# Cross attention's scores: products divided by head into two column tiles, in one run per step behind a gate on both query tiles

## The chip, the core and the metric

The kernel runs on one core of a Trainium2 chip. The core has a matrix engine (TensorE; the profile calls its matmuls PE and its weight loads PEld), a vector engine (DVE), a scalar engine (ACT), GpSimd (POOL), and SyncE (SP), which here only issues DMA transfers. The metric is the time of one execution on the device in microseconds.

## What is computed

One decoder layer on x of 16 x 64 x 512 in fp32, in three parts, each added to its input after a layer norm: attention across the batch, cross attention to a context of the same shape, and a mixture of experts (16 experts, 4 for each token, and one shared expert). The change is in the cross attention:

```python
H, KVH, HD = (32, 8, 128)
q = (hidden_states @ Wq.T).reshape(bsz, q_len, H, HD).transpose(0, 2, 1, 3)
...
q = _rmsnorm(q, q_norm_w)
...
scores = jnp.einsum('bhqd,bhkd->bhqk', q, k) * scale
scores = scores + attention_mask[:, :, :, :kv_len]
probs = jax.nn.softmax(scores.astype(jnp.float32), axis=-1).astype(q.dtype)
out = jnp.einsum('bhqk,bhkd->bhqd', probs, v)
...
return out @ Wo.T
```

There are 16 sequences of 64 queries and 64 keys, 32 query heads of 128 elements, and 8 key heads, each for a group of 4 query heads.

## The kernel before

The 1024 tokens are 8 tiles of 128, that is two sequences to a tile. Batch attention (`batch_attention`, lines 306 to 364) comes first, with the keys and values (`keys`, `values`) made in between. Cross attention follows in steps: `cross` (line 583) goes through pairs (g, u), with g one of 8 groups of 4 heads and u one of 4 pairs of tiles, so there are 32 steps. Groups 0 to 5 go one after the other; in the last eight steps groups 6 and 7 alternate, and the layer norm and the routing for the experts (`normed_pair`, `routed_pair`, `entered`) are mixed in.

A step does the following, in the order of the program:

- `softmaxed`: for both tiles of the pair, `normed_queries` scales the raw queries by their inverse root (DVE, line 479), turns them with four transposes on PE (line 482) into a bank of PSUM, and writes them to `qt` in SBUF on ACT with the norm's weight (line 484). `qt` has two buffers and is laid out as [element, sequence of the tile, head, query]. Then come the score products (line 499): for each of two pairs of heads and each of two sequences, one product whose stationary operand is `qt` of two heads x 64 queries (128 columns) and whose moving operand is the 64 keys of that sequence. Its result fills 128 partitions (two heads x 64 queries) and 64 columns of the bank `sc`. Eight products fill the 512 columns. The softmax follows on DVE and ACT (lines 504 to 515).
- `queries`: makes the raw queries of a later step, by seven products of half size in place of eight (`seven`, line 254), and their squares on ACT (line 466).
- `projected`: the output projection of the step before, again seven products (line 254).
- `attended`: turns the probabilities (line 521), multiplies them with the values (line 531, in two row tiles of 64: `64*128` in the profile) and copies the result (line 537).

An fp32 product is two records on PE, two passes each with its own weight load; a transpose is one. Tiles are handed out from pools, and the order of the instructions on each engine is laid down when the program is built, by a scheduler that takes from what is ready by its own timing the first in the program's order. So PE's order in the profile is not the program's: products of `queries` fill in where transposes or scores aren't ready. On the chip each engine then goes through its instructions in that fixed order and waits where an operand isn't there.

For comparison: batch attention's last product (line 358) writes its two halves h to two column tiles of 64 (`128*64` in the profile), and its first (line 327) works on two row tiles (`64*128`).

Of the kernel before, what the change touches and what calls it, by code (L numbers as in the profile page):

```python
# [26 lines left out]
ALU = mybir.AluOpType  # L27
AX = mybir.AxisListType

P = 128  # L30
N, C, L = 16, 64, 512
# [11 lines left out]
SURE = 32  # L43
WB = 4
ROUND = float(3 << 22)


@with_exitstack
def decoder_layer(
# [25 lines left out]
    V, S, T, G = nc.vector, nc.scalar, nc.tensor, nc.gpsimd  # L75
# [17 lines left out]
    def tr_bank():  # L93
        return bank("tr", 2)

    def sc_bank():
        return bank("sc", 3)
# [6 lines left out]
    kT = [p.tile([P, KVH // 2, NT * P], F32, tag="kT", name="kT") for p in (kvp0, kvp)]  # L104
# [372 lines left out]
    def normed_queries(g, i):  # L477
        raw = q_raw.pop((g, i))
        V.tensor_mul(raw, raw, q_rs[g, i // 2][:, i % 2, :].unsqueeze(2).to_broadcast([P, GRP, HD]))  # L479
        tp = tr_bank()  # L480
        for j in range(GRP):
            T.transpose(tp[:, j * P : (j + 1) * P], raw[:, j, :], ident)
        qt = work.tile([P, 2, GRP, C], F32, tag="qt", name="qt", bufs=2)
        S.activation(  # L484
            qt.rearrange("p b h q -> p h b q"),
            tp.rearrange("p (h b q) -> p h b q", h=GRP, b=2), AF.Copy, scale=qw_sb,
        )
        return qt

    def softmaxed(g, u):  # L490
        sp = sc_bank()
        for j in range(2):
            i = 2 * u + j
            qt = normed_queries(g, i)
            for hp in range(2):
                for b in range(2):
                    k0 = i * P + b * C
                    at = ((j * 2 + hp) * 2 + b) * C
                    T.matmul(  # L499
                        sp[:, at : at + C], qt[:, b, 2 * hp : 2 * hp + 2, :],  # L500
                        kT[g // 4][:, g % 4, k0 : k0 + C], start=True, stop=True,
                    )
        pr = work.tile([P, 8, C], F32, tag="prob", name="prob")
        V.scalar_tensor_tensor(  # L504
            pr, sp.rearrange("p (a k) -> p a k", a=8), HD**-0.5,
            mask_sb.unsqueeze(1).to_broadcast([P, 8, C]), ALU.mult, ALU.add,
        )
        mx = small.tile([P, 8], F32, tag="mx", name="mx")
        V.tensor_reduce(mx, pr, AX.X, ALU.max)
        V.tensor_sub(pr, pr, mx.unsqueeze(2).to_broadcast([P, 8, C]))  # L510
        S.activation(pr, pr, AF.Exp)
        sm = small.tile([P, 8], F32, tag="sm", name="sm")
        V.tensor_reduce(sm, pr, AX.X, ALU.add)
        V.reciprocal(sm, sm)
        V.tensor_mul(pr, pr, sm.unsqueeze(2).to_broadcast([P, 8, C]))
        return pr
# [66 lines left out]
    def cross(steps):  # L583
        for g, u in steps:
            if u == 1 and g + 2 < KVH:
                load_wq(g + 2)
            if u == 0 and g + 1 < KVH:
                load_wo(g + 1)
            pr = softmaxed(g, u)
            if g < KVH - 2:  # L590
                queries(*divmod(NT // 2 * g + u + 3, NT // 2))
            elif g == KVH - 2:
                queries(g + 1, u)
            if (g, u) == (KVH - 3, NT // 2 - 1):
                queries(g + 1, u)
            if late:
                projected(*late.pop())
            late.append((g, u, *attended(g, u, pr)))
            if g == KVH - 2 and u > 0:
                summed(u - 1)  # L600
                normed_pair(u - 1)
                if u > 1:
                    entered(u - 2, 1)
            if g == KVH - 1 and u > 0:
                routed_pair(u - 1)
                entered(u - 1, 0)
            if (g, u) == (KVH - 2, 0):
                load_shared(0)
            if (g, u) == (KVH - 2, NT // 2 - 1):
                load_shared(1)  # L610
# [78 lines left out]
    def routed_pair(u):  # L689
# [65 lines left out]
        V.tensor_scalar(col, got, 1.0 / P, (P - 1) / (2.0 * P), ALU.mult, ALU.subtract)  # L755
        V.tensor_scalar(col, col, ROUND, ROUND, ALU.add, ALU.subtract)
        row = route.tile([P, 2 * TOPK], F32, tag="row", name="row", bufs=1)
# [333 lines left out]
```

## Time and profile before

| | |
|---|---|
| median of 3 runs | 1028.77 us (1027.92 to 1031.83) |
| profiled execution | 1028.65 us, span 1026.6 us |
| PE busy | 976.3 us (95%), 4568 matmuls |
| PEld busy | 685.3 us (67%) |
| DVE busy | 542.1 us (53%) |
| ACT busy | 436.1 us (42%) |
| POOL busy | 328.7 us (32%) |
| granted TensorE clock, mean | 0.988 |

Times are from the start of the span. A row of the order of time gives start, length, engine, line, operation, out<-in, the tile of the array (rows*columns used), and in brackets the idle time before it and who ended it; xN are N records merged, so its length runs from the first start to the last end. A row of a group gives busy time and the mean ns of one, then the idle time of the engine just before. A matmul record lasts from its start to its modelled end and overlaps the next, so starts tell more than lengths.

### The profile page before, as it was taken

The numbers are of one execution on the slowest core, as the hardware profiler recorded it, in microseconds if no ns is written. First come the engines' busy times: TensorE is split into PE (matmuls) and PEld (weight loads), VectorE is DVE, ScalarE is ACT, GpSimd is POOL, SyncE is SP. The second block draws the span as 40 slices with busy tenths as digits, with TensorE's granted clock in tenths as the row PEclk, the third lists the DMA queues.
The fourth block names the chain that finished last, engine by engine and source line by source line (L and its number), as shares of the span: only waits on it lengthen the run. The fifth ranks groups of instructions, "written<-read, shape, count | busy, mean of one in ns | idle before, by whom it ended". The sixth has DMA issues, their size and how long they took to land. (4 is left out here: it accounts for less than half of the span.)

```text
span 1026.6 us, 13682 instructions
## 1 busy us (share of the span) xinstructions
PE 976.3 (95%) x4568; PEld 685.3 (67%) x4568; DVE 542.1 (53%) x1156; ACT 436.1 (42%) x1153; POOL 328.7 (32%) x356
## 2 busy tenths in 40 slices
PE   8999998999999999999999999988899999999994
PEld 3456555788888888887888887776654454454542
DVE  3555757664845756647458567688675211111110
ACT  2366662665454545545545464344220222222221
POOL 2132111421613516135235142032052444444433
PEclk9999999999999999999999999999899999999998
DMA  9120015200201102012010010000024966655764
GB/s 233 67 93 21 11 39 116 83 1 1 83 1 42 42 1 82 1 52 82 1 46 39 15 68 1 21 22 22 21 62 145 361 153 147 150 100 132 184 171 80
DMA packets 28954, 76.80 MB, mean 75 GB/s; under 512 B 4624, under 2 KB 9024, under 8 KB 26832
## 3 DMA queue, kind: packets, MB, share of 16 engines
q1 hardware_dynamic: 18160, 52.96, 15.5%
q0 software_dynamic: 10432, 22.66, 10.9%
q8 instruction: 38, 0.62, 0.3%
q14 instruction: 36, 0.29, 0.1%
q10 hardware_dynamic: 288, 0.26, 0.1%
HBM read 102.31 MB, written 14.97 MB: 114 GB/s over the span
## 5 line engine op out<-in xcount | busy, mean ns | idle before, releaser
L954 PE MATMUL sc<-w,xt 128*128 128x512 f32 x288 | 130.2, 593 | 0.3 <-ACT xt L947 0.3
L466 ACT ACTIVATE square<-qraw 128x128 f32<-128x128 f32 x256 | 79.2, 309 | 75.8 <-DVE qraw L460 37.6
L228 POOL TENSOR_TENSOR sat<-at 128x256 f32<-128x256 f32 x24 | 19.9, 828 | 211.8 <-ACT at L537 211.8
L954 PEld LDWEIGHTS sc<-w,xt 128*128 128x128 f32 x288 | 51.8, 190 | 51.7 <-issue 51.2
L959 DVE TENSOR_TENSOR z<-sc,z 128x256 f32<-128x256 f32 x36 | 15.3, 425 | 123.5 <-ACT z L958 116.7
L499 PEld LDWEIGHTS sc<-kT,qt 128*128 128x128 f32 x512 | 61.7, 191 | 17.5 <-ACT qt L484 9.3
L254 PE MATMUL mm<-wq_t,xns 128*128 128x256 f32 x256 | 70.5, 385 | 2.9 <-POOL wq_t L236 1.8
L254 PE MATMUL mm<-wo_sb,at 128*128 128x256 f32 x256 | 67.4, 388 | 5.4 <-ACT at L537 5.4
L254 PE MATMUL mm<-wq_sb,xnT 128*128 128x256 f32 x256 | 70.4, 381 | 0.0
L974 PE MATMUL mm<-w,zt 128*128 128x512 f32 x144 | 68.0, 594 | 1.5 <-DVE zt L967 1.0
L499 PE MATMUL sc<-kT,qt 128*128 128x64 f32 x512 | 69.0, 280 | 0.0
L254 PE MATMUL mm<-wo_t,sat 128*128 128x256 f32 x256 | 67.5, 384 | 0.6 <-DVE sat L229 0.6
L982 POOL DMA_INDIRECT out_dram<-y,idx x36 | 57.4, 1593 | 32.4 <-DMA out_dram<-y,idx 25.0
L936 POOL DMA_INDIRECT xg<-rows_d,idx x40 | 39.7, 994 | 82.2 <-PE tr L965 52.6
L504 DVE SCALAR_TENSOR_TENSOR prob<-sc,mask_sb 128x512 f32<-128x512 f32 x32 | 22.0, 689 | 81.4 <-PE sc L499 81.4
L479 DVE TENSOR_TENSOR qraw<-qraw,rs 128x512 f32<-128x512 f32 x64 | 62.4, 1011 | 0.6
L782 POOL DMA_INDIRECT table_d<-entry_sb,at_slot x24 | 26.0, 1084 | 108.5 <-DVE at_slot L749 102.1
L958 ACT ACTIVATE z<-sc 128x256 f32<-128x256 f32 x36 | 13.8, 384 | 104.4 <-PE sc L954 101.3
L254 PEld LDWEIGHTS mm<-wo_sb,at 128*128 128x128 f32 x256 | 48.7, 193 | 13.6 <-ACT at L537 7.2
L254 PEld LDWEIGHTS mm<-wo_t,sat 128*128 128x128 f32 x256 | 48.4, 192 | 7.3 <-POOL wo_t L237 0.7
L254 PEld LDWEIGHTS mm<-wq_t,xns 128*128 128x128 f32 x256 | 46.8, 190 | 8.7 <-POOL wq_t L236 2.0
L974 PEld LDWEIGHTS mm<-w,zt 128*128 128x128 f32 x144 | 27.1, 190 | 35.3 <-issue 32.0
(274 smaller groups left out, 2058.5 us busy)
## 6 DMA issues: line engine op xcount, KB each, us to landing
w<-in_wg_dram SPq DMA_DIRECT2D x40, 512.0 KB
w<-in_wu_dram SPq DMA_DIRECT2D x40, 512.0 KB
w<-in_wd_dram SPq DMA_DIRECT2D x40, 512.0 KB
wq_sb<-in_wq_dram SPq DMA_DIRECT2D x8, 1024.0 KB
wo_sb<-in_wo_dram SPq DMA_DIRECT2D x8, 1024.0 KB
xs<-in_x_dram SPq DMA_DIRECT2D x8, 256.0 KB
wv_sb<-in_wv_dram SPq DMA_DIRECT2D x2, 1024.0 KB
ct<-in_ctxt_dram SPq DMA_DIRECT2D x8, 256.0 KB
```

The lines of the kernel that those rows point to most:

```text
L228: engine.tensor_add(s[:, 0], a21, a22)
L254: T.matmul(dst, left[:, k, :], right[:, k, :], start=k == 0, stop=k == 1)
L466: S.activation(square, raw[:, h, :], AF.Square, accum_out=q_ss[g][:, 2 * u + j, h : h + 1])
L479: V.tensor_mul(raw, raw, q_rs[g, i // 2][:, i % 2, :].unsqueeze(2).to_broadcast([P, GRP, HD]))
L499: T.matmul(sp[:, at : at + C], qt[:, b, 2 * hp : 2 * hp + 2, :], kT[g // 4][:, g % 4, k0 : k0 + C], start=True, stop=True,)
L504: V.scalar_tensor_tensor(pr, sp.rearrange("p (a k) -> p a k", a=8), HD**-0.5, mask_sb.unsqueeze(1).to_broadcast([P, 8, C]), ALU.mult, ALU.add,
L782: G.indirect_dma_start(tables_d[q], bass.IndirectOffsetOnAxis(at_slots[u][:, q : q + 1], axis=0), entry_sb[:, 2 * u + j, k, :], None,)
L936: G.indirect_dma_start(xg, None, rows_d, bass.IndirectOffsetOnAxis(idx[:, b : b + 1], axis=0))
L954: T.matmul(hp, xt[:, d, :], w1_tiles[buffer(j)][:, :, d, :], start=(d == 0), stop=(d == DC - 1))
L959: V.tensor_mul(z, hp[:, FI:], z)
L974: T.matmul(op, zt[:, c, :], w2_tiles[buffer(j)][:, c, :], start=(c == 0), stop=(c == FI // P - 1))
L982: G.indirect_dma_start(out, bass.IndirectOffsetOnAxis(idx[:, b : b + 1], axis=0), y, None, bounds_check=NT * P - 1, oob_is_err=False, comp ...
```

## The change

```diff
+LOWEST = -3.0e38
...
     def softmaxed(g, u):
         sp = sc_bank()
-        for j in range(2):
-            i = 2 * u + j
-            qt = normed_queries(g, i)
-            for hp in range(2):
-                for b in range(2):
-                    k0 = i * P + b * C
+        qts = [normed_queries(g, 2 * u + j) for j in range(2)]
+
+        first, second = (qt[:, :, :, 0:1] for qt in qts)
+        V.scalar_tensor_tensor(first, second, LOWEST, first, ALU.is_ge, ALU.mult)
+        for hp in range(2):
+            for b in range(2):
+                for j, qt in enumerate(qts):
+                    k0 = (2 * u + j) * P + b * C
                     at = ((j * 2 + hp) * 2 + b) * C
-                    T.matmul(
-                        sp[:, at : at + C], qt[:, b, 2 * hp : 2 * hp + 2, :],
-                        kT[g // 4][:, g % 4, k0 : k0 + C], start=True, stop=True,
-                    )
+
+                    for h in range(2):
+                        T.matmul(
+                            sp[h * C : (h + 1) * C, at : at + C], qt[:, b, 2 * hp + h, :],
+                            kT[g // 4][:, g % 4, k0 : k0 + C], start=True, stop=True,
+                        )
```

Each product of two heads becomes two of one head: 64 stationary columns in place of 128, the same 64 keys as moving operand, and the result in the lower or the upper 64 partitions, which makes the two heads two column tiles. The products of both tiles of the pair come after both tiles' queries. Between them stands one DVE instruction, the gate: on one query of each head and sequence (8 elements of each partition) it multiplies the first tile's values by (second tile's value >= -3.0e38), which is 1, and writes them back in place. So the first tile's products wait for the gate and the gate waits for the second tile's `qt`; the second tile's products wait for their `qt` alone. Results and their places stay the same.

## Prediction

> **What bounds the kernel now.** I first cut the span into stages and took each engine's busy time in each. The columns are the stretch, its length, then busy time and instruction count of PE, PEld, DVE, ACT and POOL, the granted TensorE clock, the DMA share and GB/s.
>
> ```profile
> core 0: us, PE busy (x) PEld busy (x) DVE busy (x) ACT busy (x) POOL busy (x), PEclk, DMA share, GB/s
> 190.00:460.00 270.00, 266.99 (x1486) 226.91 (x1486) 164.38 (x281) 142.51 (x412) 95.35 (x106) 1.00 0.09 33
> 460.00:725.00 265.00, 249.84 (x1397) 211.30 (x1396) 185.94 (x389) 128.31 (x348) 81.23 (x78) 0.99 0.09 33
> ```
>
> Cross attention runs from 190 to about 727 us. PE is busy in 516.8 of these 535 us at full clock; DVE, the next engine, in 350. As busy ends of matmuls are modelled, I checked the order of time in one ordinary step (the lines of PE and of what it waits for):
>
> ```profile
> 506.37 0.60 PE L482 MATMUL tr<-ident,qraw 128*128 128x128 f32 x4
> ...
> 506.80 0.60 PE L254 MATMUL mm<-wq_sb,xnT 128*128 128x256 f32 x2
> ...
> 507.33 1.13 PE L531 MATMUL sc<-pt,v 64*128 64x256 f32 x8
> ...
> 508.39 1.10 PE L499 MATMUL sc<-kT,qt 128*128 128x64 f32 x8
> ...
> 509.34 0.61 PE L482 MATMUL tr<-ident,qraw 128*128 128x128 f32 x4
> ...
> 509.78 0.60 PE L254 MATMUL mm<-wq_sb,xnT 128*128 128x256 f32 x2
> ...
> 509.98 0.69 ACT L484 ACTIVATE qt<-tr,qw_sb 128x512 f32<-128x512 f32 x1 [0.36 <-PE tr L482]
> ...
> 510.21 0.59 PE L254 MATMUL mm<-wq_t,xns 128*128 128x256 f32 x2
> ...
> 510.72 0.97 PEld L499 LDWEIGHTS sc<-kT,qt 128*128 128x128 f32 x8 [0.31 <-ACT qt L484]
> 510.72 1.10 PE L499 MATMUL sc<-kT,qt 128*128 128x64 f32 x8
> ...
> 511.86 0.69 DVE L504 SCALAR_TENSOR_TENSOR prob<-sc,mask_sb 128x512 f32<-128x512 f32 x1 [5.04 <-PE sc L499]
> ```
>
> Each PE row starts as the one before drains; the step repeats every 16.58 us (L531 at 507.33 and at 523.91) without a hole. So in an ordinary step PE's own issue is the bound, and a nanosecond taken from it comes off the end. DVE meanwhile stands idle 5 us for the scores.
>
> The score products themselves, with the DVE row nearest to the gate:
>
> ```profile
> L499 PEld LDWEIGHTS sc<-kT,qt 128*128 128x128 f32 x512 | 61.7, 191 | 17.5 <-ACT qt L484 9.3 <-issue 8.0
> L499 PE MATMUL sc<-kT,qt 128*128 128x64 f32 x512 | 69.0, 280 | 0.0
> L758 DVE SCALAR_TENSOR_TENSOR row<-col,got 128x8 f32<-128x8 f32 x1 | 0.2, 156 | 0.0
> ```
>
> The 256 products of the code give 512 records, two passes each. Record by record they start 111 ns apart. A 256-wide record (L254) takes 216 ns and a 128-wide one (L482) 109, that is width times 0.84 ns, so 64 columns need 54 ns: the 128-column weight load, 107 ns, is the bound here and half the matmul slot is empty. That is what a column tile can win.
>
> **The nearest row for the new form.** Batch attention already has column tiles of 64 (L358, 128*64, alternating between the halves), with 128 moving columns. First PE's rows around it, then the first loads of that run in a window of 80 ns:
>
> ```profile
> 63.77 0.43 PE L358 MATMUL sc<-pt,qt 128*64 128x128 f32 x2
> 64.14 0.66 PE L318 MATMUL tr<-ident,xf 128*128 128x128 f32 x4
> 64.72 1.09 PE L358 MATMUL sc<-pt,qt 128*64 128x128 f32 x14
> 65.74 1.16 PE L327 MATMUL sc<-xf 64*128 64x128 f32 x16
> ```
> ```profile
> 64.72 0.20 PEld L358 LDWEIGHTS sc<-pt,qt 128*64 128x64 f32 x4 [0.16 <-ACT pt L353]
> ```
>
> Fourteen records in 1.09 - 0.27 = 0.82 us are 63 ns apiece, where one tile alone would need 109. Record by record, partners on the two halves start 7 ns apart and a pair repeats every 109 ns: both tiles run at full width at once. The four loads start at 0, 6, 55 and 61 ns: a 64-column load takes 54 ns, and the halves load at the same time; on one path the fourth would have started at 160 ns.
>
> **Part by part.**
>
> *Twice as many products, half as wide.* A step has 16 records of 128 columns now, 32 of 64 columns afterwards, 16 on each half. With load and matmul both 54 ns per tile, plus the 3 or 4 ns that L499 shows over its load, a pair takes 57 ns: 16 x 57 = 0.91 us, in place of 16 x 111 = 1.78. A rule speaks against this: the Trainium skill, "TensorE: Matmul & The Clock Gate", Part 3, "The mechanism", says that loads overlap matmuls in flight only where the row group differs, and both halves here use all 128 rows. By the rule a record would cost load plus matmul, 107 ns, the run 3.4 us and the kernel 32 x 1.9 = 60 us more (estimate). But L358 shares its rows too, and its loads start inside matmuls in flight; I take the row.
>
> *Changes of tiling.* Between L318 and L358 the start-to-start is 203 ns in place of 109, out as well as in: 94 ns. The first record of a new form also doesn't overlap its load: 160 ns in place of 109 for L318 (+0.05), 320 in place of 216 for L254 (+0.105). Now a step changes form for L531 alone; afterwards also into and out of the score run. New per step: in 0.094, first pair 0.05, out 0.09, first L254 after it 0.105, and 0.058 for transposes that come right behind L531 where the scores stood: 0.40 us. What goes: 0.08 us that L254 gives up ahead of the second half's scores (291 ns in place of 216), and the same first-record losses of L499, 2 x 0.05.
>
> *Sum of a step.* Before: 0.942 + 0.941 (the two score runs to the next row's start) + 0.075 = 1.96. After: 0.91 + 0.40 = 1.31. Saved 0.65. In the six steps whose scores already are one run of 16: 1.835 + 0.07 = 1.905 before, 1.25 after, the same 0.65. Times 32: 20.9 us.
>
> *The gate.* One DVE instruction a step, 128x8, between the second tile's L484 on ACT and the first tile's scores. Nearest row L758, 156 ns; L514, 128x8, has 192. With some 0.03 from ACT to DVE and 0.05 from DVE to PE (read at L442 to L443, and L479 to L482) it adds 0.25 us to the way from queries to scores. Queued behind it on DVE stand L504 and the softmax, which wait for these scores anyway, and in a group's first steps L479 of later tiles. As DVE waited for the scores in 25 of 32 steps (81.4 us in all), its 32 x 0.17 = 5.5 us cost DVE nothing there. On PE the L254 products fill the wait, as four do now in 509.78 to 510.72; the second tile's scores wait for ACT alone and may go ahead of the first's. Without that cover the gate costs its 0.25 us each step, 8 us. Lower end: zero, since the drain of the change of form (0.09) runs beside it; a gain is excluded. Upper end: 0.3 us in each step, 9.6. I take 0.06 a step, 2 us, nearer to the covered steps.
>
> *Where PE isn't the bound.* In the last eight steps (from 586 us) PE has about 12 us of waits for chains through DVE and ACT. There I count half: 2.6 us less. No DMA is issued or moved; both qt buffers are used in a step as before, and the softmax that follows starts at about the same point (it ends at 517.0 in the step shown, and L521, which needs it, comes at 522.5).
>
> Sum against the profiled execution (1028.65 us, of which 1026.6 are span): 20.9 - 2.6 - 2.0 = 16.3 saved. It lies 0.1 us from the median of the runs, 1028.77, so I forecast 1012.5.
>
> **Rivals.**
>
> *Slower: the pairs don't keep up.* L358 shows two loads and two matmuls in 109 ns; the change asks for that in 57, twice the rate. If PE gives out one matmul with its load no faster than about L358's own 55 to 63 ns, the halves take turns. The same skill page, Part 1, "Wait — 56ns, not 53.3ns?", has a sequencer cost of 62 ns a matmul when the hardware decoder is off, and a floor of 25 ns otherwise: by the first, 32 x 62 + 400 = 2.38 us a step, 13.5 us slower in all (estimate); by the second nothing changes. At 57.5 ns it is 2.24, 0.28 a step, 9 us slower: 1038. It decides from 49 ns a record, where 32 x 49 + 400 meets 1.96. For it: no row is denser. Against it: starts 6 and 7 ns apart at the head of each run, which no such floor allows. Chance 0.15.
>
> *Little gained: the run is late or cut up.* The order on each engine is fixed before the run from another timing than the chip's. If PE stands 0.4 us for the gate (a 1.0 us L479 ahead of it on DVE, half seen), or the run is cut in two (another 0.34 us of changes), 0.3 or less of the 0.65 is left: 32 x 0.25 = 8 us at most, with the late steps' loss some 5: 1024. For it: L479 rows of a group's start stand five together. Against it: 25 idle waits of DVE. Chance 0.17.
>
> *The gain is given back later.* The routing and expert stages (from 727 us) wait on this stage's end only, so they move with it; I see nothing that would hold them. Chance 0.03, about 1027.
>
> **How the numbers follow.** My forecast, 1012.5, has 0.65; its own range is 1006 (no losses, 20.9 saved, and a little more in the late steps) to 1019 (gate at its upper end). Cutting off the slower case and a low tail leaves 1005 to 1030. Half a per cent, 5.1 us, is about what a measurement can tell from no change. Faster by more: the 0.65 and half of the second rival, 0.74; within: 0.11; slower: 0.15.
>
> **What would show it.** In the changed profile the score rows should be 128*64, 1024 records, some 32 in one stretch of about 1.2 us (the last record's tail included), once a step; two or more stretches a step would be the second rival, 1.9 us or more the first. A step should repeat every 15.9 us. PE's idle ahead of the scores, put down to DVE, should stay under 0.1 us a step, and DVE's wait at L504 should shrink by what it waits at the gate. I am wrong if the stretch is long, if PE waits for the gate, or if other products are moved so that L521 waits for the softmax.

## The result, and the profile after

The changed kernel takes 1055.42 us (median of 6 runs, 1053.76 to 1056.35), the kernel before 1028.35 in its 6 runs beside it: a ratio of 1.0254, with a 95% interval of 1.0233 to 1.0274. The profiled execution took 1056.17 us, of which 1054.3 are span, at a mean granted clock of 0.969 (0.988 before). That is 27 us slower where I had forecast 16 us faster, and far outside my range.

In the changed code most lines of this stage stand five further down: the scores are L504 (L499 before), the scaling of the raw queries L480 (L479), their transposes L483 (L482), the copy to `qt` L485 (L484), the first softmax instruction L509 (L504), the projections' products L255 (L254), the products with the values L536 (L531), the copies of their results L542 (L537). The gate is L496.

The stages, with the columns of the table in the prediction:

```profile
190.00:460.00 270.00, 249.54 (x1654) 207.10 (x1653) 169.21 (x286) 133.73 (x389) 91.93 (x92) 0.97 0.08 28
460.00:725.00 265.00, 240.09 (x1547) 198.11 (x1545) 174.19 (x343) 120.84 (x336) 78.10 (x83) 0.95 0.10 34
```

PE is idle for 20 us of the first stretch, where it was idle for 3, and its granted clock is 0.97 and 0.95, where it was 1.00 and 0.99. The groups of the score products and of the gate (busy us, mean ns, then the idle time of the engine just before them) say for whom it stood:

```profile
L504 PE MATMUL sc<-kT,qt 128*64 128x64 f32 x1024 | 40.2, 237 | 25.7 <-DVE qt L496 25.7
L496 DVE SCALAR_TENSOR_TENSOR qt<-qt 128x8 f32<-128x8 f32 x32 | 11.9, 371 | 49.4 <-ACT qt L485 49.3
```

The tiles are as planned: 1024 records, 40.2 us of PE in place of 69.0. But PE waits 25.7 us for the gate, 26 times, where its score rows had 0.0 us of idle time ahead of them. Where that is lies in the order of time. An ordinary step first, PE's rows of one from behind the second tile's transposes to the scores (the step repeats every 16.19 us, L536 at 504.98, 521.17 and 537.36; 16.58 before):

```profile
522.72 0.60 PE L255 MATMUL mm<-wq_sb,xnT 128*128 128x256 f32 x2
523.16 1.03 PE L255 MATMUL mm<-wq_t,xns 128*128 128x256 f32 x4
524.41 1.15 PE L504 MATMUL sc<-kT,qt 128*64 128x64 f32 x32 [0.23 <-DVE qt L496]
```

All 32 records stand in one run of 1.15 us, next row at 525.49, and PE waits 0.23 us. Here the change gains. Now the second step of a group, here of group 2. First PE, then DVE:

```profile
340.23 0.55 PE L483 MATMUL tr<-ident,qraw 128*128 128x128 f32 x3 [1.08 <-DVE qraw L480]
...
343.76 0.59 PE L255 MATMUL mm<-wq_sb,xnT 128*128 128x256 f32 x2
348.13 1.97 PE L504 MATMUL sc<-kT,qt 128*64 128x64 f32 x32 [3.78 <-DVE qt L496]
350.04 2.08 PE L255 MATMUL sc<-wq_sb,xnT 128*128 128x256 f32 x4
```
```profile
338.38 1.79 DVE L480 TENSOR_TENSOR qraw<-qraw,rs 128x512 f32<-128x512 f32 x1
340.09 0.68 DVE L564 TENSOR_TENSOR acc<-mm,acc 128x512 f32<-128x512 f32 x1
340.69 6.77 DVE L480 TENSOR_TENSOR qraw<-qraw,rs 128x512 f32<-128x512 f32 x5
347.39 0.69 DVE L496 SCALAR_TENSOR_TENSOR qt<-qt 128x8 f32<-128x8 f32 x1
```

The inverse roots of three pairs come at once (`queries` forms them for pair 0 and then for pairs 1 to 3), so all six scalings become ready together, and the order laid down for DVE puts them in one lot. This step needs the first two of the six. The gate stands behind all six and runs at 347.39, though ACT has written both `qt` by 344.16 (L485 of this step: 342.88, 1.28 us for both). Before, the same lot stood on DVE (the same step, of group 3):

```profile
403.23 7.32 DVE L479 TENSOR_TENSOR qraw<-qraw,rs 128x512 f32<-128x512 f32 x5
410.47 0.68 DVE L504 SCALAR_TENSOR_TENSOR prob<-sc,mask_sb 128x512 f32<-128x512 f32 x1
```

and the scores didn't go through DVE: they started at 404.85, while the lot was running. The softmax, L504, came right behind it and found its scores done. The lot hid the scores; now it holds them.

The wait, a hole in PE's work, costs a second time, by the clock. The stretches are the wait, then three pieces of what follows it, with the columns of the stage table:

```profile
344.00:348.13 4.13, 0.35 (x2) 0.00 (x0) 4.13 (x5) 1.71 (x3) 4.05 (x5) 0.81 0.00 0
348.13:351.80 3.67, 3.67 (x36) 3.28 (x37) 1.66 (x3) 0.00 (x0) 0.60 (x1) 0.50 0.00 0
351.80:356.00 4.20, 4.20 (x17) 3.53 (x17) 1.86 (x4) 1.43 (x5) 0.00 (x0) 0.81 0.00 0
356.00:361.70 5.70, 5.70 (x29) 4.95 (x28) 3.89 (x8) 3.96 (x14) 0.00 (x0) 1.00 0.02 4
```

The granted clock is 0.50 in the first stretch behind the hole, 0.81 in the next and 1.00 in the last. Narrower windows read 1.00 up to 346.4, 0.50 from 346.6 to 353.3 and 1.00 from 353.4 on: the clock falls while PE still stands, and each 0.81 is a mean of the two. The score run takes 1.91 us to the next row there, where it takes 1.08 in the ordinary step, and the 46 records of L255 behind it take 11.65, where 46 x 0.2155 is 9.91.

The account of this one step on PE, from L526 (L521 before) to the next L526, 338.11 to 361.69: 23.58 us, 17.05 before, 6.5 more. The wait for the gate 3.85 (4.16 from the start of the last record ahead of it to the scores, where it is 0.31 without a wait), the clock 2.46 (0.83 in the scores and 1.63 in L255; 0.11 of the 1.74 there is the loss of the first record behind the scores, which the ordinary step has too: 0.97 from 525.49 to 526.46 for four records), a longer wait for the first scaling 0.83, and the tiles give back about 0.6.

The whole span, by the starts of the first softmax instruction and the first expert product (L959):

| | before | after |
|---|---|---|
| start to the first softmax of (0, 0) | 193.7 | 192.0 |
| from there to that of (6, 0): groups 0 to 5 | 407.6 | 428.6 |
| from there to the first expert product: last eight steps, routing | 200.6 | 209.0 |
| from there to the end | 224.8 | 224.7 |

Of the 21 us in the groups, the first two steps of groups 1, 2, 3 and 5 make 24.7 (33.66 each pair of steps before, 39.0 to 40.3 after); all other steps together give back 3.7. In these four groups PE waits 3.8 us for the gate in the second step, in group 4 only 1.2.

How much of the whole is the clock's can be estimated: between the first softmax and the first expert product the clock is at 0.50 for 58 us (17 before), and PE is busy in 50 of them (16 before). Half of the difference, up to 17 us of the 28, is the price of the slower clock, and the rest that of the waits less the gain of the tiles.

### The profile page after: what moved, and what is told of

The parts are those of the page before. It is cut to its first block, busy times and chain, and to the rows that moved or that the text cites. A ratio compares the mean times of both kernels' runs of the same rounds, so it can differ in the third digit from the quotient of the medians.

```text
span 1054.3 us, 14698 instructions
## 1 busy us (share of the span) xinstructions
PE 974.2 (92%) x5080; PEld 673.1 (64%) x5080; DVE 559.3 (53%) x1188; ACT 433.3 (41%) x1153; POOL 331.7 (31%) x356
## 5 line engine op out<-in xcount | busy, mean ns | idle before, releaser
L959 PE MATMUL sc<-w,xt 128*128 128x512 f32 x288 | 130.1, 593 | 0.3 <-issue 0.3
L229 POOL TENSOR_TENSOR sat<-at 128x256 f32<-128x256 f32 x24 | 20.2, 841 | 233.5 <-ACT at L542 233.5
L959 PEld LDWEIGHTS sc<-w,xt 128*128 128x128 f32 x288 | 51.8, 190 | 51.7 <-issue 51.7
L255 PE MATMUL mm<-wo_sb,at 128*128 128x256 f32 x256 | 72.5, 410 | 6.5 <-ACT at L542 4.8
L255 PE MATMUL mm<-wq_sb,xnT 128*128 128x256 f32 x256 | 73.0, 390 | 0.0
L255 PE MATMUL mm<-wo_t,sat 128*128 128x256 f32 x256 | 67.9, 386 | 3.2 <-DVE sat L230 2.8
L516 ACT ACTIVATE prob<-prob 128x512 f32<-128x512 f32 x32 | 20.1, 630 | 119.9 <-DVE prob L515 119.9
L255 PE MATMUL mm<-wq_t,xns 128*128 128x256 f32 x256 | 66.5, 380 | 2.9 <-POOL wq_t L237 1.8
L987 POOL DMA_INDIRECT out_dram<-y,idx x36 | 57.3, 1593 | 33.4 <-DMA out_dram<-y,idx 25.7
L480 DVE TENSOR_TENSOR qraw<-qraw,rs 128x512 f32<-128x512 f32 x64 | 66.2, 1069 | 0.5
L504 PE MATMUL sc<-kT,qt 128*64 128x64 f32 x1024 | 40.2, 237 | 25.7 <-DVE qt L496 25.7
L255 PEld LDWEIGHTS mm<-wo_sb,at 128*128 128x128 f32 x256 | 51.6, 205 | 16.8 <-ACT at L542 7.1
L504 PEld LDWEIGHTS sc<-kT,qt 128*64 128x64 f32 x1024 | 35.5, 148 | 38.0 <-DVE qt L496 37.0
L255 PEld LDWEIGHTS mm<-wo_t,sat 128*128 128x128 f32 x256 | 49.0, 194 | 11.2 <-POOL wo_t L236 2.1
L255 PEld LDWEIGHTS mm<-wq_t,xns 128*128 128x128 f32 x256 | 48.6, 191 | 10.2 <-POOL wq_t L237 2.2
```

The source lines that it names most:

```text
L229: engine.tensor_add(s[:, 0], a21, a22)
L255: T.matmul(dst, left[:, k, :], right[:, k, :], start=k == 0, stop=k == 1)
L504: T.matmul(sp[h * C : (h + 1) * C, at : at + C], qt[:, b, 2 * hp + h, :], kT[g // 4][:, g % 4, k0 : k0 + C], start=True, stop=True,)
L959: T.matmul(hp, xt[:, d, :], w1_tiles[buffer(j)][:, :, d, :], start=(d == 0), stop=(d == DC - 1))
L987: G.indirect_dma_start(out, bass.IndirectOffsetOnAxis(idx[:, b : b + 1], axis=0), y, None, bounds_check=NT * P - 1, oob_is_err=False, comp ...
```

## The experiments

In each the time is the median, with the ratio to the kernel before on the same chip (1028.4 to 1029.9 there) and its 95% interval. The stages are those of the table above.

| | us | ratio | groups 0 to 5 | last eight, routing |
|---|---|---|---|---|
| before | 1028.35 | | 407.6 | 200.6 |
| after: tiles, one run, gate | 1055.42 | 1.0254 (1.0233 to 1.0274) | 428.6 | 209.0 |
| e1: after without its gate (two runs) | 1022.73 | 0.9950 (0.9929 to 0.9971) | 401.3 | 200.0 |
| e2: gate, no tiles | 1089.49 | 1.0574 (1.0522 to 1.0627) | 454.0 | 218.2 |
| e3: gate ahead of later scalings | 1030.36 | 1.0003 (0.9982 to 1.0024) | 402.2 | 211.6 |
| e4: tiles, each tile by itself, no gate | 1014.54 | 0.9867 (0.9840 to 0.9894) | 395.6 | 197.7 |
| e5: tiles, one run by PE's order | 1023.62 | 0.9952 (0.9935 to 0.9968) | 401.0 | 199.1 |
| e6: after, with roots by pair | 1021.45 | 0.9918 (0.9894 to 0.9942) | 393.3 | 209.5 |
| e7: after, with its hole filled | 1057.70 | 1.0262 (1.0221 to 1.0302) | 429.5 | 207.2 |
| e8: e5, copies behind the queries | 1015.22 | 0.9858 (0.9837 to 0.9879) | 394.0 | 200.7 |
| e9: e8, last eight steps as e4 | 1011.33 | 0.9833 (0.9808 to 0.9858) | 395.7 | 197.2 |

**e1, the gate taken out.** The products stay in the one loop behind both tiles' queries; nothing else holds them together as one run.

```diff
-        first, second = (qt[:, :, :, 0:1] for qt in qts)
-        V.scalar_tensor_tensor(first, second, LOWEST, first, ALU.is_ge, ALU.mult)
```

> The changed kernel without its gate; the products of both tiles still come after both tiles' queries. PE's order, read from the built program, then has two score runs a step (4 records, then 28, with four other products between) in place of one. Queue theory (the gate's DVE instruction stands behind the scalings of later queries, and PE waits for it): no PE wait for DVE ahead of the scores; the second run costs about 0.34 us of changes of form, so 0.65 - 0.34 = 0.31 us a step is saved against the kernel before: about 1019 us. Tile theory (the divided products, their changes of form and a lower clock that they bring cost the time): as slow as the change or slower, 1055 us or more.

1022.73, so the gate costs 32.7 us by the medians; in the profiled executions, 35.6 apart, 27.3 are in the groups and 9.0 at the end. The divided products without it are a gain. It is still 10 us short of my forecast, since an ordinary step takes 16.24 us and not 15.93. As the expectation said, the scores come in two runs: 4 records (L502 at 503.35 in one such step), four of L255, then 28 (504.68), without any wait of PE. Against e8, which has one run and no wait, the step is 0.34 us longer, the price that the prediction had for a run cut in two.

**e2, the gate without the division.** The loop and the gate of the change, with the undivided products of before.

```diff
-                    for h in range(2):
-                        T.matmul(
-                            sp[h * C : (h + 1) * C, at : at + C], qt[:, b, 2 * hp + h, :],
+                    T.matmul(
+                        sp[:, at : at + C], qt[:, b, 2 * hp : 2 * hp + 2, :],
```

> The changed kernel with the undivided products of before (two heads, 128 columns), so the gate and the one run alone. Queue theory: the same waits for the gate as in the change, and the run of 16 records takes 1.84 us where the divided one takes 1.08, with fewer changes of form: some 0.7 us a step more than the change, about 1075 us. Tile theory: back near the kernel before, 1028 to 1038 us.

1089.49, 14 us more than expected, and PE waits 27.8 us for the gate, 26 times, about as in the change. An ordinary step takes 16.90 us, 0.32 over before, where the divided one takes 16.19. So behind the gate the division is worth 34 us of the total, more than the 21 at stake by PE's issue. The ordinary steps' 0.71 makes 23 of it over 32 steps. The clock can make the rest: from the first softmax to the first expert product it is at 0.50 for 85 us here, with PE busy in 76, where the change has 58 and 50, which is up to 13 us (estimate). The direction is plain: the tiles are no part of the loss.

**e3, the gate ahead of the scalings that the step doesn't need.** Each scaling is ordered behind the gate of the step before it.

```diff
     def normed_queries(g, i):
         raw = q_raw.pop((g, i))
-        V.tensor_mul(raw, raw, ...)
+        with tc.issue_after(gates[-1]) if gates else ExitStack():
+            V.tensor_mul(raw, raw, ...)
...
-        V.scalar_tensor_tensor(first, second, LOWEST, first, ALU.is_ge, ALU.mult)
+        gate_op = V.scalar_tensor_tensor(first, second, LOWEST, first, ALU.is_ge, ALU.mult)
+        gates.append(getattr(gate_op, "ins", gate_op))
```

> The changed kernel with one constraint on DVE's order: the scalings of a step's queries are issued behind the gate of the step before, so that at most the step's own two scalings stand ahead of a gate. All instructions are the same. Queue theory: the long waits of 4 us go, the short ones of 0.3 us stay; an ordinary step takes 16.2 us against 16.58 before, so about 1028 - 32 x 0.39 = 1016 us, up to 1024 where the roots of the queries come late. Tile theory: no change, 1055 us.

The groups did what was expected: 402.2 us, a group's four steps 66.5 in place of 72.2 (66.8 before), and PE's wait for the gate falls from 25.7 to 11.1 us. The total did not, by 6 us: 1030.36. The last eight steps lose 11 us against before, and there DVE's rows show another queue ahead of the gate, then PE's rows of the same place:

```profile
609.95 1.29 DVE L229 TENSOR_TENSOR sat<-at 128x256 f32<-128x256 f32 x1 [1.35 <-ACT at L546]
...
613.98 1.48 DVE L231 TENSOR_TENSOR sat<-at,sat 128x256 f32<-128x256 f32 x1
615.38 1.23 DVE L499 SCALAR_TENSOR_TENSOR qt<-qt 128x8 f32<-128x8 f32 x1
```
```profile
616.66 1.84 PE L508 MATMUL sc<-kT,qt 128*64 128x64 f32 x32 [2.77 <-DVE qt L499]
```

In groups 6 and 7 the four sums of the output (`left_sums`) are on DVE and not on POOL. They stand in line ahead of the gate, which is L499 in this kernel, and PE stands for 2.77 us. The gate itself takes 1.23 us for 8 elements. In the change it is the same place, the first step of group 7: the four sums, the gate, and a wait of 2.79 us. From the first softmax of group 6 to the last of group 7 PE is idle for 20.2 us there (12.4 before), 4.1 of them at the gate, at a granted clock of 0.92 (1.00 before). e1 shows that the gate brings the loss at the end; that it is these sums which hold it is read from the rows, as no run moves them.

**e6, the roots taken pair by pair.** The other way to the same end: the scalings aren't ready all at once.

```diff
-        done = (0, 1, 2, 3) if g == KVH - 1 else (0, 3)
+        done = (0, 1, 2, 3)
```

> The changed kernel, gate and all, with the inverse roots of the queries made for each pair of tiles in all groups, not in two lots (first pair, then three at once) in groups 0 to 6. So DVE never has six scalings to do at once. It costs ACT up to two more table loads of 1.28 us in a step. Queue theory: no wait of 4 us for the gate is left, every ordinary step takes about 16.2 us, 1014 to 1022 us. If the long waits come from something else in the gate: 1045 us or more.

1021.45, at the upper end of the expectation. With the gate still there the groups are 35 us shorter than in the change and even shorter than in e1; the wait for the gate is 11.7 us. The last eight steps are as slow as in the change (209.5). So two different edits shorten the line ahead of the gate, and both take the loss in the groups away and leave the loss at the end, where the line is another one. e3 changes DVE's order alone. e6 also spreads the work on the roots over the steps, and as its groups are shorter than those of e1, which has no gate, that must be worth something by itself; no run has it without the gate.

**e7, the hole filled.** In the second step of groups 1 to 5, eight more products, whose result is overwritten, ahead of the scores. They are extra work; nothing is left out.

```diff
+        if u == 1 and 0 < g < KVH - 2:
+            for _ in range(8):
+                T.matmul(sp[:, :256], ident, xnT[:, 0, :256], start=True, stop=True)
```

> The changed kernel with eight idle products (16 records, 3.4 us; their result is overwritten) ahead of the scores in the five steps in which PE waits 4 us for the gate (second pair of groups 1 to 5). The scheduler puts them in place of four real products, which then come after the scores: 1.7 us more work each behind the gate, and some 2 us of waiting left in front. If the hole in PE's work is what lowers the granted clock (0.68 in the 3.7 us after it, 2.5 us lost a time), the clock stays at 1.00 there and the two cancel: 1050 to 1056 us. If the clock falls for another reason: 5 x 1.7 more, 1064 us.

The total, 1057.70, lies between the two cases of the expectation and can't be told from the change. The step itself shows the clock's part. PE's rows of the same step, then the stretch behind the wait, with the columns of the stage table:

```profile
343.01 3.62 PE L498 MATMUL sc<-xnT,ident 128*128 128x256 f32 x16
348.68 1.15 PE L508 MATMUL sc<-kT,qt 128*64 128x64 f32 x32 [2.05 <-DVE qt L500]
```
```profile
349.00:352.70 3.70, 3.70 (x44) 3.30 (x39) 2.65 (x5) 1.32 (x2) 0.28 (x1) 1.00 0.00 0
```

The scores start 10.02 us after the step's first transpose in both kernels, as DVE's line is the same. The hole is 2.05 us, and the clock stays at 1.00. From the scores to the next step's transposes it is 12.84 us, in the change 13.56. The filler had also pushed eight records of L255 behind the scores (54 there, 46 in the change), 8 x 0.2155 = 1.72 us; without these it would be 11.12. So the clock costs the change 2.44 us in this step, as in the account (2.46). In the total this is not seen: in the profiled execution the kernel is 2.0 us ahead of the change by the second step of group 2 (counted from the first softmax), still 1.9 in group 3, and 0.9 behind at the end of group 5. The traces show where that goes. In group 4 the change has a wait of only 1.2 us to fill, so there most of the filler is extra work: the first two steps take 37.82 us, in the change 35.56. In group 5 the same hole of 2.06 us was followed by a fall of the clock after all (0.50 from 565.7 to 568.9): 40.75 us, in the change 40.27.

**e4, tile by tile.** The kernel before with the division alone: no gate, and each tile's products behind its own queries.

```diff
-                    T.matmul(
-                        sp[:, at : at + C], qt[:, b, 2 * hp : 2 * hp + 2, :],
+                    for h in range(2):
+                        T.matmul(
+                            sp[h * C : (h + 1) * C, at : at + C], qt[:, b, 2 * hp + h, :],
```

> The kernel before with its products divided by head and nothing else: each query tile's products stay where they stood, so a step has two divided runs of 16 records, and there is no gate. Prices of the prediction: two runs of 8 pairs at 57 ns, each with its changes of form; against 1.96 us before about 2 x 0.46 + 0.40 + 0.34 = 1.66, so 0.30 us a step, 1019 us. If the divided form costs more than that where it comes in two runs: 1028 us or more.

1014.54, better than expected and than e1, though its scores come in two runs a step. A run of 16 records takes 0.61 us to the next row and an ordinary step 16.04, so the second run costs 0.14 us over e8's 15.90 and not the 0.34 that the expectation had. The first run comes right behind L531, where PE changed its form in any case.

**e5, one run without a gate.** The order is only told to PE: the second tile's products first, then the first tile's.

```diff
+        last = None
+        for j in (1, 0):
+            with tc.issue_after(last) if last is not None else ExitStack():
...
+                            op = T.matmul(...)
+            last = getattr(op, "ins", op)
```

> The divided products without the gate, kept in one run by PE's order alone: the second tile's products are written first and the first tile's are issued behind them. No DVE instruction is added. Queue theory, with the prediction's prices for the tiles: 0.65 us a step saved, an ordinary step 15.93 us in place of 16.58, 1008 to 1013 us. Tile theory: 1040 us or more.

1023.62, like e1 and 11 to 16 us slower than I expected. PE waits 8.2 us ahead of the scores, 24 times, now for ACT. PE's and ACT's rows of one ordinary step:

```profile
501.80 1.07 ACT L542 COPY at<-sc 128x512 f32<-128x512 f32 x2 [0.81 <-PE sc L536]
...
502.57 0.59 PE L255 MATMUL mm<-wq_t,xns 128*128 128x256 f32 x2
502.76 0.70 ACT L485 ACTIVATE qt<-tr,qw_sb 128x512 f32<-128x512 f32 x1
...
503.51 1.15 PE L503 MATMUL sc<-kT,qt 128*64 128x64 f32 x32 [0.35 <-ACT qt L485]
```

The second tile's `qt` (L485) stands on ACT behind the two copies of the values' products (L542), 1.07 us. Before, the first tile's scores lay between L531 and the second tile's transposes and gave ACT 0.94 us for these copies. With all scores at the end that cover is gone, and only four records of L255 lie between the transposes and the scores.

**e8, the copies behind the queries.** e5, and in groups 0 to 5 the copies to `at` are issued behind the next step's second `qt`.

```diff
+        def copied():
+            with tc.issue_after(turned[-1]) if g < KVH - 2 else ExitStack():
+                for b in range(2):
+                    S.copy(at[:, :, b * C : (b + 1) * C], ...)
...
             pr = softmaxed(g, u)
+            if late:
+                late.append(late.pop()())
```

> The divided products in one run by PE's order, without a gate, and in groups 0 to 5 the two copies of the attention output on ACT are issued behind the second tile's queries. In the run with PE's order alone PE stood 0.42 us a step for ACT ahead of the scores, since those copies (1.07 us) come first. If that is what is left of the prediction's 0.65 us, an ordinary step falls from 16.31 to about 15.9 us and the time by some 22 x 0.38 = 8 us, to 1015 us. If the copies are needed as early as they are: no gain, 1023 us, and PE waits for the copies further on.

1015.22, as expected, and the ordinary step takes 15.90 us. PE's rows around the scores of a step, the third of group 2:

```profile
351.62 0.59 PE L255 MATMUL mm<-wq_t,xns 128*128 128x256 f32 x2
352.14 1.15 PE L506 MATMUL sc<-kT,qt 128*64 128x64 f32 x32
353.23 0.70 PE L255 MATMUL mm<-wq_t,xns 128*128 128x256 f32 x2
```

The scores start without an idle time ahead of them, and the next row of L255 starts at 353.76. From 16.58 to 15.90 is 0.68 a step.

**e9, both orders.** e8 for groups 0 to 5, and in the last eight steps tile by tile as in e4, since from the first softmax of group 6 to the last of group 7 e4 takes 121.9 us and e8 127.1 (124.9 before). The expectation means this stretch, though it names the first expert product as its end.

```diff
+        one_run = g < KVH - 2
...
-        for j in (1, 0):
-            with tc.issue_after(last) if last is not None else ExitStack():
+        for j in (1, 0) if one_run else (0, 1):
+            if not one_run:
+                qts[j] = normed_queries(g, 2 * u + j)
+            with tc.issue_after(last) if one_run and last is not None else ExitStack():
```

> Groups 0 to 5 as in the run with the copies behind (one run of scores, no gate), the last eight steps as in the run tile by tile (two runs). In their profiles the time from the softmax of the first of the last eight steps to the first expert product is 127.1 us with one run and 121.9 with two, while an ordinary step takes 15.90 with one run and 16.04 with two. If one run costs the last steps that time because both tiles' queries come late there: 1010 to 1012 us. If the difference of the two is scatter between executions: 1015 us as both.

1011.33, a ratio of 0.9833 (0.9808 to 0.9858): faster than both kernels, with the tiles of the change, its single run in 24 of 32 steps, and no gate. Its interval overlaps those of e4 and e8, so that it is the best of the three isn't shown.

## Why the prediction was wrong

**The step that failed is the price of the gate.** I wrote: "As DVE waited for the scores in 25 of 32 steps (81.4 us in all), its 32 x 0.17 = 5.5 us cost DVE nothing there", and "I take 0.06 a step, 2 us". The gate costs 32.7 us (change against e1). Three things went wrong in that one step.

- I priced the instruction and not the line that it joins. Where DVE stands idle the gate is cheap: 0.30 us of PE's time in an ordinary step, which was the upper end of my bounds. The steps in which it doesn't were the ones to price, and the count of 25 pointed at them: among the seven steps before in which L504 follows without an idle time are the second steps of groups 1, 2, 3 and 5 (410.47 above is one) and the first of group 7, the five in which PE now waits 3.8 and 2.8 us for the gate. I had the lot of L479 before my eyes ("L479 rows of a group's start stand five together") and still took it as "a 1.0 us L479 ahead of it on DVE, half seen", 0.4 us. The gate waits for the whole lot: 3.85 us of PE in group 2. e3 and e6 both thin out that lot, each in its own way, and in both the loss of the groups is gone.
- The end of the stage was bounded by the waits of before. There the line ahead of the gate is made of the sums of the output (by the rows of e3 and of the change), and the stage, for which I counted a gain of 2.6, lost 8.4.
- A hole in PE also costs clock. The sum had no term for it; e7 shows 2.44 us in one step, and over the stage it is up to 17 us (the estimate above).

**The cover that I named was gone.** "On PE the L254 products fill the wait, as four do now" holds for the gate's own 0.25 us, but moving the first tile's scores to the end took away what had covered ACT's copies. That, and not the gate, is the 0.41 us a step between e5 (16.31) and e8 (15.90). e1 has no such wait; what it lacks to e8 is the cut in its run. In the ordinary step of the change the two waits overlap: PE stands 0.30 us there and 0.42 in e5, but in the change two more records of L255, 0.43 us, are set ahead of the scores (six, four in e5), so the gate's own part is 0.31 us.

**The slower rival was another mechanism.** "The pairs don't keep up" is refuted: 32 records take 1.08 us to the next row; less the 0.05 and the 0.094 that I priced for the first pair and the way out, that is 0.938, or 58.6 ns for each of 16 pairs, where I took 57. Neither the loads' rule nor a floor of 62 ns a record shows. "Little gained: the run is late or cut up" named the right place. But it gave PE a wait of 0.4 us, 13 us over 32 steps, and so left a gain of 5 to 8 us; the gate's price, 32.7 us, is more than all that the tiles could win, and so falls on the other side.

**What held.** The tiles are worth 0.68 us in an ordinary step (e8), forecast 0.65; the changes of form cost what batch attention's rows said (in e8's rows two records of L255 take 0.52 us ahead of the scores and 0.53 behind them, in place of 0.43: 0.09 and 0.10, priced at 0.094 and 0.105); two shorter runs still gain (e4). The experts move with the end of the stage: 224.8 us before and 224.7 after. The forecast of 1012.5 is near what the tiles give where nothing waits for the gate (e9, 1011.33), but that agreement is of another kernel, in which ACT's order is changed too.

**What stays open.** Whether the sums of the output are all that holds the gate at the end of the stage; what the roots taken pair by pair (e6) are worth without a gate; and whether the clock is really the rest of e2's 34 us.

## What to carry to other kernels

An instruction that only orders others waits in its engine's line like any other: price it by what stands ahead of it in the worst step, not by its own duration or by the engine's mean idle time. Where only one engine's order matters, tell the order to that engine: e5 and e8 get the same single run without a gate. And when work is moved to make one long run, ask what its old place had covered; here it was the copies of another engine.

## What the hardware showed beyond that

- **The clock falls after short holes, but not after each.** In narrow windows the granted clock of these traces is 0.50 or 1.00, and the stretches at 0.50 last 3.4 us or two to four times that. The wait of 3.8 us in the change was followed by 5 to 6 us at 0.50 in groups 1, 2 and 5, but in group 3 only by 3.4 us, which began 1.3 us behind its end. In e3 a hole of 2.77 us was followed by 0.54 over 3.7 us. In e7 one of 2.05 or 2.06 us brought no fall in groups 1 to 3, and one of 2.06 us brought 3.4 us at 0.50 in group 5. The Trainium skill, "TensorE: Matmul & The Clock Gate", section "HAM oscillation — how this bites in real kernels", asks for no gaps of over about 3.4 us; the holes of e3 and e7 lie under that and still brought it down. In one execution the falls lie whole multiples of 3.41 us apart (in the change at 274.85, 346.53, 421.62 and 561.57: 21, 22 and 41 of them). That fits a clock which is set at fixed points of time, so that the place of a hole between them decides; no run here tests it.
- **DVE is slower beside POOL.** The gate, 8 elements a partition, took 166 ns at the least and 1225 at the most; the six times that it ran without a POOL instruction beside it the median was 170, the 26 others 276. The scaling L480 took 0.68 us in the median of the 20 alone and 1.21 in that of the 44 beside POOL. Both have two operands in SBUF, and this agrees with the Trainium skill, "SBUF — State Buffer", section "Who interferes with whom", which says that such an instruction contends with a GpSimd instruction that reads SBUF. It is also a part of why the gate waits so long: at 0.68 us each the last five scalings would take 3.4 us (estimate), and they take 6.8.
